# The y product of a Mamba block on small TensorE tiles, with a compact decay matrix and a new layout of PSUM

## The chip, the core and the metric

The kernel runs on one core of one Trainium2 chip. The metric is the device time of one execution in microseconds, as the median of three runs. The profile is of one execution of its own.

A core has five engines with a queue each. TensorE (PE in the profile) does matmuls and loads their weights (PEld). VectorE (DVE) and ScalarE (ACT) do elementwise work and can read PSUM, the memory that matmuls write. GpSimd (POOL) does elementwise work in SBUF alone. SyncE (SP) issues most DMAs. Each queue is served in order; an instruction waits for semaphores of other engines, and what stands behind it waits as well.

## The reference

The input x has 64 sequences of 32 tokens with 512 channels. The first layer adds to x the result of a Mamba block on a conditioned copy of x; the second adds a routed feed-forward layer. The change lies in the Mamba block. Cut to that:

```python
proj = hidden @ in_proj_w.T                  # gate 4096, x 4096, B 1024, C 1024, dt 64
xBC  = silu(causal_conv4(proj.xBC) + conv_bias)
dt   = softplus(dt + dt_bias);  dA = exp(-dt * exp(A_log))
def step(state, t):                          # 64 heads of 64 channels, 8 groups, state size 128
    state = state * dA[t] + dt[t] * x[t] * B[t]
    y[t]  = state @ C[t]
y = y + x * D
y = y * rsqrt(mean_over_group(y * y) + eps) * norm_weight * silu(gate)
out = y @ out_proj_w.T
```

As a sequence has only 32 tokens, the kernel does not step. For each sequence and head it makes a 32 by 32 matrix of decays from token s to token t, multiplies it by the 32 by 32 matrix of B[s]·C[t], and multiplies x by the product.

## The kernel before

The 64 sequences are four tiles T of 16 sequences, so 512 tokens. Channels lie on the partitions and tokens along the free dimension, four blocks bg of 128 tokens (four sequences of 32). For each T the eight groups g are worked through: 32 passes i. All large matmuls are split: each operand is a rounded part (hi) and a rest (lo) in fp32r, and `mm_split` (L159) does hi·hi, lo·hi and hi·lo, 12 matmuls of 128 x 128 x 512 for a product with four blocks of contraction.

The main loop (L689) does the work of three passes at once. For pass i it projects ten chunks of 128 channels (`chunk`, L307: B, C, four of x, four of the gate z): 12 matmuls into a bank with tag "mm", then on ACT and DVE a convolution of four taps (L331, L337), silu (L345), and for x a transpose of 32 x 32 blocks into xs (L349). `x_move` (L404) moves xs by 16 DMAs into xt, with the 128 tokens of a block on the partitions. For pass j = i - 1 it makes the decay matrix: `scan` (L367) on POOL (L372) and DVE (L379); `gram` (L384), 16 matmuls of B and C, each 32 x 32 in the output, whose result DVE multiplies into bd (L397); and `yunit` (L415) four times, the y product. bd is [128 tokens, 4 blocks, 8 heads, 128 tokens]: for each block and head a 128 x 128 matrix whose four diagonal blocks of 32 x 32 are filled (L398) and whose rest was set to zero once (L221). A y product is 8 matmuls with 128 rows of contraction: 4 blocks by 2 heads ("half", 64 channels each).

After the y product DVE adds D·x (L431), ACT squares (L435), POOL sums the squares over c (L439), DVE multiplies by the norm weight and the gate (L442), and ACT and DVE split the result into yhi and ylo (L448, L449). For pass o = i - 2, `sumsq` and `sumsq2` (L453, L462) sum squares over channels and tokens (L457, L459, four small matmuls at L468, L472 on DVE, a power on POOL at L474), `outp` (L493) does the output projection of each block bg by 12 matmuls, and `outp_end` (L509) adds it, scaled, into acc on DVE (L514). `wo_load` (L479) loads and splits the output weights, `w_load` and `w_split` (L287, L295) those of the chunks, with the rests made on POOL (L302, L491). At the first group of a T there are also `cond` (L169, conditioned input), `dt_stage` (L228) and, before it, `attend` (L109). After the last pass follows the feed-forward layer (a convolution, 16 transposes into c2, routing, 16 dense products).

The tile framework decides the order on each engine: it reorders the program's instructions by its own estimates, keeps data dependencies by tile, and sets the semaphores. PSUM has 8 banks, given by tag: three "mm" (chunks), three "yo" (y products, output blocks, and later transposes and half of the dense products), two "gs" (gram and all small results). A tag's banks are used in turn; a writer waits until the bank's last tile has been read.

Of the kernel before, what the change touches and what calls it, by code (L numbers as in the profile page):

```python
# [32 lines left out]
def mamba_block_kernel(  # L33
# [63 lines left out]

    h1_ps = ps.tile([P, NB], F32, tag="gs", name="h1_ps", bufs=2)
# [3 lines left out]
    h2_ps = ps.tile([P, NB], F32, tag="gs", name="h2_ps", bufs=2)  # L102
    nc.tensor.matmul(h2_ps, lhsT=k1["w1"], rhs=h1, start=True, stop=True)
# [5 lines left out]
    def attend(T):  # L109
# [3 lines left out]
        )  # L113
        lg_ps = ps.tile([P, NBG, 8], F32, tag="gs", name=f"lg_ps{T}", bufs=2)
        for bg in range(NBG):
# [53 lines left out]
    def cond(T):  # L169
        acc = acc_of[T]  # L170
        hid = sb.tile([P, 2, KC, TOK], F32R, tag="hid", name=f"hid{T}", bufs=1)
        hid_hi, hid_lo = hid[:, 0], hid[:, 1]
        hid_of[T] = (hid_hi, hid_lo)
        h_of = []
        for k in range(KC):
            h_ps = ps.tile([P, TOK], F32, tag="mm", name=f"h_ps{T}_{k}", bufs=3)
            for bg in range(NBG):
                nc.tensor.matmul(
                    h_ps[:, 128 * bg : 128 * bg + 128],
                    lhsT=acc[:, bg, 128 * k : 128 * k + 128],  # L180
                    rhs=abd[:, bg, :],
                    start=True,
                    stop=True,
                )
            if k == 0:
                b_ps = ps.tile([P, TOK], F32, tag="yo", name=f"b_ps{T}", bufs=3)
# [16 lines left out]
    bd = sb.tile([P, NBG, HPG, P], F32, tag="bd", name="bd", bufs=1)  # L203
    ctxT = const.tile([P, NB], F32, tag="ctxT", name="ctxT")
# [5 lines left out]
    def setup_rest():  # L210
        wdt_s = sb.tile([P, KC, P], F32, tag="dt", name="wdt_s", bufs=1)
        nc.sync.dma_start(out=wdt_s, in_=wdt)
        nc.scalar.copy(wdt_hi, wdt_s)
        nc.vector.tensor_tensor(wdt_lo, wdt_s, wdt_hi.bitcast(F32), ALU.subtract)
        ac = const.tile([P, 2], F32, tag="ac", name="ac")
        nc.vector.tensor_scalar(ac[:, 0:1], k2["alog"], 88.0, None, ALU.min)
        nc.vector.tensor_scalar(ac[:, 1:2], k2["alog"], 88.0, 0.0, ALU.subtract, ALU.max)
        nc.vector.tensor_scalar(ac[:, 1:2], ac[:, 1:2], 80.0, None, ALU.min)
        nc.scalar.activation(e1, ac[:, 0:1], AF.Exp)
        nc.scalar.activation(e2, ac[:, 1:2], AF.Exp)  # L220
        nc.gpsimd.memset(bd, 0.0)  # L221
        ct_ps = ps.tile([P, NB], F32, tag="gs", name="ct_ps", bufs=2)
        nc.tensor.matmul(ct_ps, lhsT=k2["cw"], rhs=k1["condT"], start=True, stop=True)
        nc.vector.tensor_scalar(ctxT, ct_ps, k2["fs"], None, ALU.add)
# [3 lines left out]
    def dt_stage(T):  # L228
# [11 lines left out]
        v, e, s, q, m = (w[:, n] for n in range(5))  # L240
        for r, c in ((slice(0, 64), slice(0, 256)), (slice(64, 128), slice(256, 512))):
            nc.vector.tensor_scalar(v[r], d_ps[r, c], dtb_s[r], None, ALU.add)
        nc.scalar.activation(e, v, AF.Abs)
# [16 lines left out]
        for f in range(2):  # L260
# [3 lines left out]
            )  # L264
        t_ps = ps.tile([P, 2, 2, 64], F32, tag="gs", name=f"t_ps{T}", bufs=2)
        for k in range(2):
# [40 lines left out]
    def chunk(i, c):  # L307
# [38 lines left out]
        if kind == "x":  # L346
            if k == 0:
                st["xs"] = sb.tile([P, NBG, 4, 4, L], F32, tag="xs", name=f"xs{i}", bufs=1)
            nc.vector.transpose(  # L349
                st["xs"][:, :, k].rearrange("p g b c -> p g (b c)"),  # L350
                t.rearrange("p (g x) -> p g x", g=NBG),
            )
# [31 lines left out]
    def gram(i):  # L384
        st = state[i]
        g_ps = ps.tile([P, NBG, L], F32, tag="gs", name=f"g_ps{i}", bufs=2)
        for bg in range(NBG):
            for q in range(4):
                c = slice(128 * bg + 32 * q, 128 * bg + 32 * q + 32)
                nc.tensor.matmul(  # L390
                    g_ps[32 * q : 32 * q + 32, bg, :],
                    lhsT=st[("B", 0)][:, c], rhs=st[("C", 0)][:, c], start=True, stop=True,
                )
        dec = st.pop("dec")
        for q in range(4):
            r = slice(32 * q, 32 * q + 32)
            nc.vector.tensor_tensor(  # L397
                bd[r, :, :, r],  # L398
                dec[r],
                g_ps[r].unsqueeze(2).to_broadcast([32, NBG, HPG, L]),  # L400
                ALU.mult,
            )

    def x_move(i):  # L404
        xs = state[i].pop("xs")
        xt = sb.tile([P, NBG, 4, 4, L], F32, tag="xt", name=f"xt{i}", bufs=2)
        for q in range(4):
            for b in range(4):
                nc.sync.dma_start(
                    out=xt[32 * b : 32 * b + 32, :, :, q, :],  # L410
                    in_=xs[32 * q : 32 * q + 32, :, :, b, :],
                )
        state[i]["xt"] = xt.rearrange("p g c q x -> p g c (q x)")

    def yunit(i, c):  # L415
        g = i % NG
        st = state[i]
        xt = st["xt"]
        y_ps = ps.tile([P, TOK], F32, tag="yo", name=f"y_ps{i}_{c}", bufs=3)
        for bg in range(NBG):  # L420
            for half in range(2):
                nc.tensor.matmul(  # L422
                    y_ps[64 * half : 64 * half + 64, 128 * bg : 128 * bg + 128],
                    lhsT=xt[:, bg, c, 64 * half : 64 * half + 64],
                    rhs=bd[:, bg, 2 * c + half, :],
                    start=True,
                    stop=True,
                )
        cc = 4 * g + c
        y = sb.tile([P, TOK], F32, tag="y", name=f"y{i}_{c}", bufs=3)  # L430
        nc.vector.scalar_tensor_tensor(  # L431
            y, st.pop(("x", c)), dsk_s[:, cc : cc + 1], y_ps, ALU.mult, ALU.add
        )
# [15 lines left out]
        nc.vector.tensor_tensor(  # L449
            st["ylo"][:, c, :], z, st["yhi"][:, c, :].bitcast(F32), ALU.subtract  # L450
        )

    def sumsq(i):  # L453
# [8 lines left out]
    def sumsq2(i):  # L462
        st = state[i]
        part = st.pop("part")
        s_ps = ps.tile([P, NBG], F32, tag="gs", name=f"s_ps{i}", bufs=2)
        pv = part.rearrange("p (g b) -> p b g", b=4)
        for q in range(4):
# [25 lines left out]
    def outp(i, bg):  # L493
# [80 lines left out]
    def c2_tiles(T):  # L574
# [3 lines left out]
        if T == 2:  # L578
            t = sb.tile([P, 2, 4, TOK], F32R, tag="bd", name="c2_2", bufs=1)
            return t[:, 0], t[:, 1]  # L580
        tags = (("acc", 2), ("xt", 2)) if T == 1 else (("yhi", 1), ("ylo", 1))
# [26 lines left out]
    def c2_xpose(j):  # L608
        T, jj = divmod(j, 4)
        c2 = ffn.pop(("c2", j))  # L610
        if jj == 0:
            c2_of[T] = c2_tiles(T)
        o = ps.tile([P, 4, 4, L], F32, tag="yo", name=f"ctp{j}", bufs=3)
        for b in range(4):
# [23 lines left out]
    def route2(T):  # L638
        ls = ffn.pop(("ls", T))
        t_ps = ps.tile([P, NBG, 64], F32, tag="gs", name=f"lt{T}", bufs=2)  # L640
        for bg in range(NBG):
# [162 lines left out]
    dense(2)  # L804
    cnt_ps = ps.tile([64, 2], F32, tag="gs", name="cnt_ps", bufs=2)
    for n in range(16):
# [136 lines left out]
```

## Time and profile before

| | us |
|---|---|
| median of three runs | 1697.29 (1696.21 to 1698.06) |
| span of the profiled execution, first to last instruction | 1693.9 |
| PE busy | 1623.6 |
| DVE busy | 1394.7 |
| POOL busy | 973.9 |
| ACT busy | 791.5 |
| mean granted TensorE clock, share of full | 0.987 |

The profiled execution's own time is not listed apart from its span, which lies 3.4 us under the median of the runs. The page sums busy time by engine, then follows the chain of work that ended last, then lists groups of equal instructions: line, engine, operation, out<-in, shapes and count, then busy us and mean ns of one, then idle time ahead of it and what ended that. The timeline lists instructions in order of time, equal neighbours merged: start, length in us, engine, line. A line of the waits gives who waited for whom, the sum in us, how often, and the longest. A line of the windows gives the stretch and its length, then busy time (count of instructions) of PE, PEld, DVE, ACT and POOL, the granted clock, the busy share of DMA and GB/s.

### The profile page before, as it was taken

How to read it: one execution, taken by the hardware profiler on the slowest of the kernel's cores; microseconds unless marked ns; L12 is line 12 of the kernel's file. 1: busy time of each engine (PE TensorE's matmuls, PEld its weight loads, DVE VectorE, ACT ScalarE, POOL GpSimd, SP SyncE). 2: the span in 40 equal slices, each digit the busy share in tenths (PEclk: the TensorE clock that was granted, in tenths of full speed). 3: DMA queues.
4: the chain of work that ended last, by engine and by line, in shares of the span. 5: the costliest groups of instructions: out<-in, count | busy, mean ns of one | idle time of the engine just before them, and what ended most of it. 6: DMA issues, size and time to landing. Idle time of an engine off the chain costs nothing.

```text
span 1693.9 us, 26413 instructions
## 1 busy us (share of the span) xinstructions
PE 1623.6 (96%) x9427; PEld 1260.1 (74%) x9427; DVE 1394.7 (82%) x1820; ACT 791.5 (47%) x1333; POOL 973.9 (57%) x767
## 2 busy tenths in 40 slices
PE   6899999999999999999999999999999999999999
PEld 5677777777777777777777777777777777777677
DVE  7688888888988788877988878888888878787658
ACT  4444554445545454544645444444644444454330
POOL 5356755654576665564576555665556566665620
PEclk9999999999999999999999999999999999999999
DMA  5344543443555343443554344444344444444333
GB/s 164 91 112 112 135 100 95 111 109 90 110 150 145 92 121 99 111 115 88 125 128 137 100 116 101 108 116 121 86 134 105 120 115 106 118 129 119 100 114 124
DMA packets 376739, 193.70 MB, mean 114 GB/s; under 512 B 285920, under 2 KB 311264, under 8 KB 376608
## 3 DMA queue, kind: packets, MB, share of 16 engines
q1 hardware_dynamic: 375328, 187.81, 43.3%
q0 software_dynamic: 1280, 4.20, 0.6%
q8 instruction: 75, 1.23, 0.3%
q14 instruction: 56, 0.46, 0.1%
HBM read 149.46 MB, written 8.91 MB: 93 GB/s over the span
## 4 chain that ended last, share of the span: by engine, by line
PE 51%; DVE 20%; POOL 12%; issue 8%; DMA 5%; ACT 2%; SPq 1%; POOLq 0%; DVEq 0%; ACTq 0%
PE mm L164 22%; PE o L164 15%; PE y_ps L422 5%; POOL wlo L302 4%; DVE bd L397 3%; POOL wolo L491 3%; POOL y L439 3%; PE fo L164 3%; DVE ylo L449 2%; DMA wor<-in_wout_dram 2%; DVE x L337 2%; DVE z L442 2%; PE cv L164 2%; DMA w<-in_win_dram 1%; DVE src L379 1%
## 5 line engine op out<-in xcount | busy, mean ns | idle before, releaser
L164 PE MATMUL mm<-hid,whi 128*128 128x512 f32 x2560 | 700.8, 403 | 13.5 <-DVE x L337 5.4
L302 POOL TENSOR_TENSOR wlo<-w,whi 128x512 fp32r<-128x512 f32 x320 | 465.8, 1472 | 339.6 <-ACT whi L301 281.0
L164 PEld LDWEIGHTS mm<-hid,whi 128*128 128x128 f32 x2560 | 468.9, 189 | 139.3 <-issue 29.8
L164 PE MATMUL mm<-hid,wlo 128*128 128x512 f32 x1280 | 352.3, 397 | 4.2 <-POOL wlo L302 4.2
L337 DVE SCALAR_TENSOR_TENSOR x<-mm,pack,x 128x496 f32<-128x496 f32 (+2 forms) x384 | 270.2, 708 | 48.2 <-ACT x L331 42.9
L164 PEld LDWEIGHTS mm<-hid,wlo 128*128 128x128 f32 x1280 | 241.9, 189 | 63.9 <-POOL wlo L302 6.8
L491 POOL TENSOR_TENSOR wolo<-wor,wohi 128x512 fp32r<-128x512 f32 x128 | 207.1, 1636 | 11.8 <-ACT wohi L490 10.7
L301 ACT CAST whi<-w 128x512 fp32r<-128x512 f32 x320 | 191.8, 611 | 14.4 <-DMA w<-in_win_dram 10.9
L449 DVE TENSOR_TENSOR ylo<-z,yhi 128x512 fp32r<-128x512 f32 x128 | 143.6, 1122 | 47.3 <-ACT yhi L448 46.1
L442 DVE SCALAR_TENSOR_TENSOR z<-y,pack,z 128x512 f32<-128x512 f32 x128 | 176.4, 1378 | 2.2 <-DVE y L431 0.6
L372 POOL TENSOR_TENSOR src<-dtt,pack 128x256 f32<-128x256 f32 x128 | 75.2, 619 | 165.4 <-DVE bd L397 165.1
L422 PE MATMUL y_ps<-bd,xt 128*64 128x128 f32 x2048 | 165.7, 280 | 1.2 <-DVE acc L514 0.5
L422 PEld LDWEIGHTS y_ps<-bd,xt 128*64 128x64 f32 x2048 | 123.3, 136 | 50.8 <-issue 39.3
L439 POOL TENSOR_TENSOR y<-y,y 128x512 f32<-128x512 f32 x96 | 150.5, 1568 | 16.4 <-ACT y L435 16.3
L397 DVE TENSOR_TENSOR bd<-src,g_ps 32x1024 f32<-32x1024 f32 x128 | 155.3, 1213 | 2.2
L164 PE MATMUL o<-wohi,yhi 128*128 128x512 f32 x512 | 143.9, 400 | 7.8 <-DVE acc L514 4.1
L164 PE MATMUL o<-wohi,ylo 128*128 128x512 f32 x512 | 143.7, 397 | 7.8 <-DVE ylo L449 7.3
L331 ACT ACTIVATE x<-mm,pack 128x512 f32<-128x512 f32 x128 | 99.1, 774 | 96.5 <-PE mm L164 96.5
L328 ACT ACTIVATE z<-mm 128x512 f32<-128x512 f32 x128 | 76.4, 596 | 144.7 <-DVE ylo L449 133.1
L164 PE MATMUL o<-wolo,yhi 128*128 128x512 f32 x512 | 138.8, 393 | 0.0
L345 ACT ACTIVATE x<-x 128x512 f32<-128x512 f32 x128 | 80.2, 628 | 123.7 <-DVE x L337 123.2
L514 DVE SCALAR_TENSOR_TENSOR acc<-o,r,acc 128x512 f32<-128x512 f32 x128 | 93.0, 745 | 46.6 <-POOL r L474 29.7
(190 smaller groups left out, 1755.0 us busy)
## 6 DMA issues: line engine op xcount, KB each, us to landing
w<-in_win_dram SPq DMA_DIRECT2D x320, 256.0 KB, 3.0
wor<-in_wout_dram SPq DMA_DIRECT2D x128, 256.0 KB, 3.1
xt<-xs SPq DMA_DIRECT2D x512, 64.0 KB, 2.3
da<-da SPq DMA_DIRECT2D x128, 128.0 KB, 4.0
acc<-in_x_in_dram SPq DMA_DIRECT2D x4, 1024.0 KB, 7.3
x<-acc POOLq DMA_DIRECT2D x16, 256.0 KB, 2.8
pr<-x SPq DMA_DIRECT2D x64, 64.0 KB, 2.0
x1s<-x SPq DMA_DIRECT2D x16, 256.0 KB, 2.7
```

What stands on the lines that cost most here:

```text
L164: nc.tensor.matmul(o, lhsT=a(k), rhs=b(k), start=j == 0, stop=j == last)
L301: nc.scalar.copy(hi, w)
L302: nc.gpsimd.tensor_tensor(lo, w, hi.bitcast(F32), ALU.subtract)
L331: nc.scalar.activation(t, o, AF.Identity, bias=convb_s[:, cc : cc + 1], scale=convw_s[:, cc, 3:4])
L337: nc.vector.scalar_tensor_tensor(tv[:, :, d:], ov[:, :, : L - d], convw_s[:, cc, 3 - d : 4 - d], tv[:, :, d:], ALU.mult, ALU.add,)
L397: nc.vector.tensor_tensor(bd[r, :, :, r], dec[r], g_ps[r].unsqueeze(2).to_broadcast([32, NBG, HPG, L]), ALU.mult,)
L422: nc.tensor.matmul(y_ps[64 * half : 64 * half + 64, 128 * bg : 128 * bg + 128], lhsT=xt[:, bg, c, 64 * half : 64 * half + 64], rhs=bd[:, b ...
L439: nc.gpsimd.tensor_tensor(y2, st["y2"], y2, ALU.add)
L442: nc.vector.scalar_tensor_tensor(z, y, nw_s[:, cc : cc + 1], z, ALU.mult, ALU.mult)
L449: nc.vector.tensor_tensor(st["ylo"][:, c, :], z, st["yhi"][:, c, :].bitcast(F32), ALU.subtract)
L491: nc.gpsimd.tensor_tensor(lo[:, k, :], w, hi[:, k, :].bitcast(F32), ALU.subtract)
L514: nc.vector.scalar_tensor_tensor(acc[:, bg, :], o, st["r"][:, bg : bg + 1], acc[:, bg, :], ALU.mult, ALU.add)
```

## The change

1. The y product of a block and head is four matmuls, one for each sequence q of the block, with 32 rows of contraction and 32 columns: 32 matmuls per `yunit` where there were 8. Row group q of the array and column half "half" make eight tiles of 32 x 64.
2. The four row groups write to four different banks, so the result of one `yunit` lies in a quarter (128 columns) of each of four banks. Token order follows: q runs slowest in the chunk tokens (hid, B, C, x, z, y), and yhi and ylo are put back into the old order when they are written.
3. bd is gone. DVE multiplies the gram into the decay matrix in place, by one operation of 128 partitions in place of four of 32. The decay matrix gets two buffers (src).
4. PSUM: one tile "quad" of four banks holds y products and output blocks (block bg in bank bg), and by turns (`bank()`) what else had tag "yo". "gs" has one bank where it had two.
5. In the feed-forward part, c2 of tile 2 takes the buffer of xs and a new one, c2x, as bd is gone.

```diff
+    quad = ps.tile([P, 4, TOK], F32, tag="quad", name="quad", bufs=1)
+    turn = [0]
+
+    def bank():
+        turn[0] = (turn[0] + 1) % 4
+        return quad[:, turn[0], :]
...
-            nc.vector.tensor_tensor(h_sb, h_ps, cb_t, ALU.add)
+            nc.vector.tensor_tensor(
+                h_sb.rearrange("p (q g t) -> p g q t", q=4, g=NBG),
+                h_ps.rearrange("p (g q t) -> p g q t", q=4, g=NBG),
+                cb_t.rearrange("p (g q t) -> p g q t", q=4, g=NBG),
+                ALU.add,
+            )
...
-        nc.gpsimd.memset(bd, 0.0)
...
-                st["xs"] = sb.tile([P, NBG, 4, 4, L], F32, tag="xs", name=f"xs{i}", bufs=1)
+                st["xs"] = sb.tile([P, 4, NBG, 4, L], F32, tag="xs", name=f"xs{i}", bufs=1)
...
-        src = sb.tile([P, NBG, HPG, L], F32, tag="src", name=f"src{i}", bufs=1)
+        src = sb.tile([P, NBG, HPG, L], F32, tag="src", name=f"src{i}", bufs=2)
...
-        g_ps = ps.tile([P, NBG, L], F32, tag="gs", name=f"g_ps{i}", bufs=2)
+        g_ps = ps.tile([P, NBG, L], F32, tag="gs", name=f"g_ps{i}", bufs=1)
...
-        dec = st.pop("dec")
-        for q in range(4):
-            r = slice(32 * q, 32 * q + 32)
-            nc.vector.tensor_tensor(
-                bd[r, :, :, r],
-                dec[r],
-                g_ps[r].unsqueeze(2).to_broadcast([32, NBG, HPG, L]),
-                ALU.mult,
-            )
+        dec = st["dec"]
+        nc.vector.tensor_tensor(
+            dec, dec, g_ps.unsqueeze(2).to_broadcast([P, NBG, HPG, L]), ALU.mult
+        )
...
-        y_ps = ps.tile([P, TOK], F32, tag="yo", name=f"y_ps{i}_{c}", bufs=3)
+        yv = quad.rearrange("p q (c g t) -> p q c g t", c=4, g=NBG)
         for bg in range(NBG):
-            for half in range(2):
-                nc.tensor.matmul(
-                    y_ps[64 * half : 64 * half + 64, 128 * bg : 128 * bg + 128],
-                    lhsT=xt[:, bg, c, 64 * half : 64 * half + 64],
-                    rhs=bd[:, bg, 2 * c + half, :],
-                    start=True,
-                    stop=True,
-                )
+            for q in range(4):
+                r = slice(32 * q, 32 * q + 32)
+                for half in range(2):
+                    nc.tensor.matmul(
+                        yv[64 * half : 64 * half + 64, q, c, bg, :],
+                        lhsT=xt[r, bg, c, 64 * half : 64 * half + 64],
+                        rhs=m[r, bg, 2 * c + half, :],
+                        start=True,
+                        stop=True,
+                    )
...
-        nc.scalar.copy(st["yhi"][:, c, :], z)
+        hi, lo = (
+            st[k][:, c, :].rearrange("p (g q t) -> p q g t", g=NBG, q=4) for k in ("yhi", "ylo")
+        )
+        zv = z.rearrange("p (q g t) -> p q g t", g=NBG, q=4)
+        nc.scalar.copy(hi, zv)
...
-        o = ps.tile([P, DM], F32, tag="yo", name=f"o{i}_{bg}", bufs=3)
+        o = quad[:, bg, :]
...
-        tg = ("mm", "yo")[(j + (lo > 0)) % 2]
-        o = ps.tile([P, hi - lo], F32, tag=tg, name=f"fo{j}_{lo}", bufs=3)
+        if (j + (lo > 0)) % 2:
+            o = bank()[:, : hi - lo]
+        else:
+            o = ps.tile([P, hi - lo], F32, tag="mm", name=f"fo{j}_{lo}", bufs=3)
```

The rest of the diff adapts indices and views to the new token order, and sets `bufs=1` for the other tiles with tag "gs".

More of the change, by code (lines that the diff above doesn't have):

```diff
@@ L96, in mamba_block_kernel @@
     convb_s, dsk_s, nw_s, dtb_s = k2["convb"], k2["dsk"], k2["nw"], k2["dtb"]
-    h1_ps = ps.tile([P, NB], F32, tag="gs", name="h1_ps", bufs=2)
+    h1_ps = ps.tile([P, NB], F32, tag="gs", name="h1_ps", bufs=1)
     nc.tensor.matmul(h1_ps, lhsT=k1["w0"], rhs=k1["condT"], start=True, stop=True)
@@ L101, in mamba_block_kernel @@
     nc.scalar.activation(h1, h1_ps, AF.Gelu, bias=k1["b0"])
-    h2_ps = ps.tile([P, NB], F32, tag="gs", name="h2_ps", bufs=2)
+    h2_ps = ps.tile([P, NB], F32, tag="gs", name="h2_ps", bufs=1)
     nc.tensor.matmul(h2_ps, lhsT=k1["w1"], rhs=h1, start=True, stop=True)
@@ L113, in attend @@
         )
-        lg_ps = ps.tile([P, NBG, 8], F32, tag="gs", name=f"lg_ps{T}", bufs=2)
+        lg_ps = ps.tile([P, NBG, 8], F32, tag="gs", name=f"lg_ps{T}", bufs=1)
         for bg in range(NBG):
@@ L185, in cond @@
             if k == 0:
-                b_ps = ps.tile([P, TOK], F32, tag="yo", name=f"b_ps{T}", bufs=3)
+                b_ps = bank()
                 nc.tensor.matmul(
@@ L201, in cond @@
             )
-    bd = sb.tile([P, NBG, HPG, P], F32, tag="bd", name="bd", bufs=1)
     ctxT = const.tile([P, NB], F32, tag="ctxT", name="ctxT")
@@ L220, in setup_rest @@
         nc.scalar.activation(e2, ac[:, 1:2], AF.Exp)
-        nc.gpsimd.memset(bd, 0.0)
-        ct_ps = ps.tile([P, NB], F32, tag="gs", name="ct_ps", bufs=2)
+        ct_ps = ps.tile([P, NB], F32, tag="gs", name="ct_ps", bufs=1)
         nc.tensor.matmul(ct_ps, lhsT=k2["cw"], rhs=k1["condT"], start=True, stop=True)
@@ L240, in dt_stage @@
         v, e, s, q, m = (w[:, n] for n in range(5))
-        for r, c in ((slice(0, 64), slice(0, 256)), (slice(64, 128), slice(256, 512))):
-            nc.vector.tensor_scalar(v[r], d_ps[r, c], dtb_s[r], None, ALU.add)
+        dv = d_ps.rearrange("p (q f g t) -> p f g q t", q=4, f=2, g=2)
+        for r, f in ((slice(0, 64), 0), (slice(64, 128), 1)):
+            nc.vector.tensor_scalar(
+                v[r].rearrange("p (g q t) -> p g q t", g=2, q=4), dv[r, f], dtb_s[r], None, ALU.add
+            )
         nc.scalar.activation(e, v, AF.Abs)
@@ L264, in dt_stage @@
             )
-        t_ps = ps.tile([P, 2, 2, 64], F32, tag="gs", name=f"t_ps{T}", bufs=2)
+        t_ps = ps.tile([P, 2, 2, 64], F32, tag="gs", name=f"t_ps{T}", bufs=1)
         for k in range(2):
@@ L347, in chunk @@
             if k == 0:
-                st["xs"] = sb.tile([P, NBG, 4, 4, L], F32, tag="xs", name=f"xs{i}", bufs=1)
+                st["xs"] = sb.tile([P, 4, NBG, 4, L], F32, tag="xs", name=f"xs{i}", bufs=1)
             nc.vector.transpose(
-                st["xs"][:, :, k].rearrange("p g b c -> p g (b c)"),
-                t.rearrange("p (g x) -> p g x", g=NBG),
+                st["xs"][:, :, :, k].rearrange("p b g c -> p (b g) c"),
+                t.rearrange("p (n t) -> p n t", t=L),
             )
@@ L385, in gram @@
         st = state[i]
-        g_ps = ps.tile([P, NBG, L], F32, tag="gs", name=f"g_ps{i}", bufs=2)
+        g_ps = ps.tile([P, NBG, L], F32, tag="gs", name=f"g_ps{i}", bufs=1)
         for bg in range(NBG):
             for q in range(4):
-                c = slice(128 * bg + 32 * q, 128 * bg + 32 * q + 32)
+                c = slice(128 * q + 32 * bg, 128 * q + 32 * bg + 32)
                 nc.tensor.matmul(
@@ L410, in x_move @@
                     out=xt[32 * b : 32 * b + 32, :, :, q, :],
-                    in_=xs[32 * q : 32 * q + 32, :, :, b, :],
+                    in_=xs[32 * q : 32 * q + 32, b],
                 )
@@ L417, in yunit @@
         st = state[i]
-        xt = st["xt"]
-        y_ps = ps.tile([P, TOK], F32, tag="yo", name=f"y_ps{i}_{c}", bufs=3)
+        xt, m = st["xt"], st["dec"]
+        yv = quad.rearrange("p q (c g t) -> p q c g t", c=4, g=NBG)
         for bg in range(NBG):
-            for half in range(2):
-                nc.tensor.matmul(
-                    y_ps[64 * half : 64 * half + 64, 128 * bg : 128 * bg + 128],
-                    lhsT=xt[:, bg, c, 64 * half : 64 * half + 64],
-                    rhs=bd[:, bg, 2 * c + half, :],
-                    start=True,
-                    stop=True,
-                )
+            for q in range(4):
[8 more added lines that the diff above has]
+                    )
         cc = 4 * g + c
@@ L431, in yunit @@
         nc.vector.scalar_tensor_tensor(
-            y, st.pop(("x", c)), dsk_s[:, cc : cc + 1], y_ps, ALU.mult, ALU.add
+            y.rearrange("p (q x) -> p q x", q=4),
+            st.pop(("x", c)).rearrange("p (q x) -> p q x", q=4),
+            dsk_s[:, cc : cc + 1],
+            quad[:, :, 128 * c : 128 * c + 128],
+            ALU.mult,
+            ALU.add,
         )
@@ L447, in yunit @@
             st["ylo"] = sb.tile([P, 4, TOK], F32R, tag="ylo", name=f"ylo{i}", bufs=1)
-        nc.scalar.copy(st["yhi"][:, c, :], z)
-        nc.vector.tensor_tensor(
-            st["ylo"][:, c, :], z, st["yhi"][:, c, :].bitcast(F32), ALU.subtract
-        )
+        hi, lo = (
+            st[k][:, c, :].rearrange("p (g q t) -> p q g t", g=NBG, q=4) for k in ("yhi", "ylo")
+        )
+        zv = z.rearrange("p (q g t) -> p q g t", g=NBG, q=4)
+        nc.scalar.copy(hi, zv)
+        nc.vector.tensor_tensor(lo, zv, hi.bitcast(F32), ALU.subtract)
     def sumsq(i):
@@ L464, in sumsq2 @@
         part = st.pop("part")
-        s_ps = ps.tile([P, NBG], F32, tag="gs", name=f"s_ps{i}", bufs=2)
-        pv = part.rearrange("p (g b) -> p b g", b=4)
+        s_ps = ps.tile([P, NBG], F32, tag="gs", name=f"s_ps{i}", bufs=1)
+        pv = part.rearrange("p (b g) -> p b g", b=4)
         for q in range(4):
@@ L578, in c2_tiles @@
         if T == 2:
-            t = sb.tile([P, 2, 4, TOK], F32R, tag="bd", name="c2_2", bufs=1)
-            return t[:, 0], t[:, 1]
+            return tuple(
+                sb.tile([P, 4, TOK], F32R, tag=tg, name=f"c2_2_{tg}", bufs=1)
+                for tg in ("xs", "c2x")
+            )
         tags = (("acc", 2), ("xt", 2)) if T == 1 else (("yhi", 1), ("ylo", 1))
@@ L612, in c2_xpose @@
             c2_of[T] = c2_tiles(T)
-        o = ps.tile([P, 4, 4, L], F32, tag="yo", name=f"ctp{j}", bufs=3)
+        o = bank().rearrange("p (b f o) -> p b f o", b=4, f=4)
         for b in range(4):
@@ L639, in route2 @@
         ls = ffn.pop(("ls", T))
-        t_ps = ps.tile([P, NBG, 64], F32, tag="gs", name=f"lt{T}", bufs=2)
+        t_ps = ps.tile([P, NBG, 64], F32, tag="gs", name=f"lt{T}", bufs=1)
         for bg in range(NBG):
@@ L804, in mamba_block_kernel @@
     dense(2)
-    cnt_ps = ps.tile([64, 2], F32, tag="gs", name="cnt_ps", bufs=2)
+    cnt_ps = ps.tile([64, 2], F32, tag="gs", name="cnt_ps", bufs=1)
     for n in range(16):
@@ L815, in mamba_block_kernel @@
     dense(3)
-    r_ps = ps.tile([P, DM], F32, tag="gs", name="r_ps", bufs=2)
+    r_ps = ps.tile([P, DM], F32, tag="gs", name="r_ps", bufs=1)
     nc.tensor.matmul(r_ps, lhsT=crep, rhs=oh, start=True, stop=True)
```

## The prediction

> **What bounds the kernel now.** I read the page's first part, then its chain. TensorE (PE) is busy 96% of the span, VectorE (DVE) 82%, and no other engine comes near.
>
> ```profile
> PE 1623.6 (96%) x9427; PEld 1260.1 (74%) x9427; DVE 1394.7 (82%) x1820; ACT 791.5 (47%) x1333; POOL 973.9 (57%) x767
> PE 51%; DVE 20%; POOL 12%; issue 8%; DMA 5%; ACT 2%; SPq 1%; POOLq 0%; DVEq 0%; ACTq 0%
> ```
>
> The first row does not prove PE the bound, since ends of matmuls are modelled. The timeline of PE alone does: matmul follows matmul.
>
> ```profile
> 819.15 1.09 PE L422 MATMUL y_ps<-bd,xt 128*64 128x128 f32 x16
> 820.17 1.19 PE L164 MATMUL mm<-hid,whi 128*128 128x512 f32 x4
> ...
> 823.15 1.09 PE L422 MATMUL y_ps<-bd,xt 128*64 128x128 f32 x16
> ...
> 835.17 0.46 PE L390 MATMUL g_ps<-C,B 128*32 128x32 f32 x32
> 835.56 1.20 PE L164 MATMUL mm<-hid,whi 128*128 128x512 f32 x4
> ```
>
> Read start to start: a y product takes 820.17 - 819.15 = 1.02 us (16 records, two per fp32 matmul), y product plus chunk 4.00, a gram 0.39 for 32 records. A chunk elsewhere takes 2.79, an output product (outp) 2.73, both read in the same answer. One pass (one group of one token tile) is then 6 x 2.79 + 4 x 4.00 + 4 x 2.73 + 0.4 for the gram + 0.3 for the sums of squares = 44.4 us of PE. The windows between sums of squares of successive passes show 46.2 and 45.7, with DVE busy 39.0 and 37.2:
>
> ```profile
> 500.94:547.10 46.16, 45.85 (x273) 35.72 (x272) 39.01 (x47) 23.80 (x40) 31.21 (x23) 1.00 0.48 129
> 692.30:738.00 45.70, 45.61 (x274) 35.53 (x273) 37.17 (x47) 22.37 (x38) 26.56 (x21) 1.00 0.46 119
> ```
>
> From the first to the last sum of squares there are 31 passes in 1591.0 - 111.8 us, 47.7 each (conditioning, dt stage and attention at the tile boundaries included). So PE sets the pace, and DVE, in strict order and nearly as full, makes the 2 to 3 us of stalls. The timeline of all engines shows how late it runs:
>
> ```profile
> 499.92 1.09 PE L164 MATMUL o<-wolo,yhi 128*128 128x512 f32 x4
> ...
> 506.41 0.15 DVE L472 TENSOR_SCALAR var<-s_ps 128x4 f32<-128x4 f32 x1
> ...
> 506.64 1.03 POOL L474 TENSOR_TENSOR r<-var,mhalf 128x4 f32<-128x4 f32 x1 [1.60 <-DVE var L472]
> ...
> 507.71 0.75 DVE L514 SCALAR_TENSOR_TENSOR acc<-o,r,acc 128x512 f32<-128x512 f32 x1 [1.15 <-POOL r L474]
> ```
>
> The first output block is done on PE at 501.0 and added into acc at 508.5, 7.5 us later. PE did not care: block 1 went into another bank of three. That is the cover which the change removes.
>
> **The change, part by part.**
>
> ```profile
> L397 DVE TENSOR_TENSOR bd<-src,g_ps 32x1024 f32<-32x1024 f32 x128 | 155.3, 1213 | 2.2
> L422 PE MATMUL y_ps<-bd,xt 128*64 128x128 f32 x2048 | 165.7, 280 | 1.2 <-DVE acc L514 0.5
> POOL src L372 <- DVE bd L397: 165.1, 27, 9.4
> ```
>
> *y product.* Per unit 8 matmuls of 128 rows and 128 columns become 32 of 32 rows and 32 columns, 16 records become 64, on 8 array tiles instead of 2. The nearest row is the gram: 32 columns, four tiles of 32 columns, 32 records in 0.39 us, so 12.2 ns a record, or 49 ns for a round of four tiles. The new unit has 8 rounds of 8 tiles. Low end: a round costs as in the gram, 8 x 49 ns = 0.39 us. High end from that row: 64 x 12.2 ns = 0.78. Weights are 64 columns wide, twice the gram's, so I take nearer the high end, 0.70, a gain of 0.32 us per unit, 128 units: 41 us. A rule speaks against it: "TensorE: Matmul & The Clock Gate" of the Trainium skill ("Wait — 56ns, not 53.3ns?") says that start-to-start never falls below about 25 ns however few columns. By the rule a unit is 64 x 25 = 1.6 us, a loss of 0.58 x 128 = 74 us. The gram, 12.2 ns a record, is half that floor, so I follow the row; but no row here has four row groups at once, so the rule's end stays in the range.
>
> *bd.* Four DVE operations of 32 partitions (1.213 us each) become one of 128 partitions with the same 1024 elements per partition: 3 x 1.213 = 3.64 us of DVE less per pass, 116 us in all. In itself it moves nothing, since PE is the bound; it makes DVE earlier. The bd memset (3.5 us of POOL, once) goes.
>
> *src with two buffers.* POOL no longer stands blocked up to 9.4 us behind bd with the weight splits queued behind it. PE waited 11 us for such splits in all, so 0 to 11 us; I take 5.
>
> *PSUM.* The built program shows that every writer of quad waits for the last reader of quad, whichever bank: output block 2 waits for the addition of block 1, y product c+1 for the DVE read of y product c, the first y product for the addition of block 3. Behind the waiting matmul all of PE's queue stands. Three banks in rotation become one. A quad user mostly has one chunk (2.79 us) between it and the next, and in that time DVE must come round. In 9 of the 32 passes the new order puts blocks 1, 2, 3 side by side; each of those two joints costs a bare round trip, about 0.15 + 0.75 (L514) + 0.15 less the normal pitch, 0.9 us: 9 x 1.8 = 16 us.
>
> For the other passes I step through one by hand, in the built order, with the rows' durations (z 1.38, ylo 1.12, the rest about 0.7, bd 1.21). New PE time is 44.4 - 4 x 0.32 = 43.1. Between y reads 1 and 2, DVE has ylo, transpose, z, ylo, read: 5.0 us and 0.7 of waiting for ACT's yhi, against 3.7 on PE; the third y product waits about 0.6, the fourth 0.4. From the end of the fourth y product to the first addition DVE has its backlog 2.5, read 0.73, z 1.38, a wait for POOL's add 0.9, transpose and sum 1.4, ylo 1.1, bd 1.2, six conv steps 4.3, var 0.15, r 1.2, addition 0.75 = 15.6, while PE reaches output block 1 after chunk 3.0, gram 0.4, two chunks 5.6, block 0 2.7, sums 0.3, chunk 2.8 = 14.8: 0.9 us (with joints) of stall. Blocks 2 and 3 have slack. With 0.3 for DMA waits now spread over eight matmuls of the first y product: 2.2 us.
>
> *gs with one buffer.* Three times (passes 9, 17, 25) the gram stands directly behind the sums of squares and must wait for var: about 1.5 us each, 5 us. Elsewhere 8 us of PE lie between: nothing. If that cover went, each would cost the same 1.5.
>
> *Token order.* xs, h_sb, dt, y, yhi and ylo are written with runs of 32 elements. L397 wrote such runs at 1213 ns for 1024 elements, the pace of plain rows, so nothing; the DMA of x keeps its count and its 128-byte destination runs.
>
> Sum per pass: 43.1 + 2.2 stalls, against about 46.0: -0.7 x 32 = -22; joints +16; gram waits +5; POOL -5; the longer passes (47 to 55 us, where DVE's backlog is worst) should give back another 0.5 us on some 25: -13. Together -19 us on the span of 1693.9. The median of runs is 1697.3, 3.4 above that span; so 1678.
>
> **Rivals.** *The lock-step costs more than the matmuls give* (slower). One mechanism: DVE does not come round within one chunk, at the joints y to y and at the first addition. It decides from 2.9 us of stall per pass on (46.0 - 43.1); I have 2.2. At 4 us the sum moves by 1.8 x 32 = 58: 1736. For it: additions are 7.5 us late now; z and ylo show 1.77 us in places. Against: 3.64 us less on DVE. *Small tiles meet a floor per record* (slower): by the rule above 115 us off the sum, 1793; break-even near 13 ns a record. *DVE's relief wins* (faster): if POOL is not in the way z and ylo show 0.75 and 0.7, the lock-step fits, and stalls are under 1 us: 1678 - 1.5 x 32 = 1630. That the change does nothing on PE can also be: if four row groups take turns for weights, the unit stays near 1.0 and the time near 1719.
>
> **How the numbers follow.** My sum (1655 to 1694) 0.45, of which 0.07 lies within 0.2% of before (3.4 us, about what a measurement of this kernel can tell from no change); faster rival 0.13; lock-step 0.27, of which 0.02 within 0.2%; floor or no gain on PE 0.15. Faster 0.51, same 0.09, slower 0.40. Range 1635 to 1745: it leaves out the rule's end and the far ends of both others.
>
> **What would show it.** The y rows should start 64 records within 0.7 us (over 1.0: wrong). bd's row should be x32 at 1.2 us. Among PE's waits y and quad behind DVE L431 and L514 (their new lines) should come up with some 50 to 90 us; over 100 us means that the lock-step rival holds. DVE should be near 1280 us busy. Wrong I am above all if DVE's lag at the joints differs by 1 us, 32 us of time.

## The result, and the profile after

The changed kernel takes 1766.11 us (median of four runs, 1764.15 to 1767.61) against 1696.94 (of four too, 1696.21 to 1698.06): 1.0412 times the time before, with an interval of 1.0397 to 1.0427. It is slower by 69 us; 1678 was predicted, with a range up to 1745. The profiled execution has a span of 1762.4 us, 68.5 above that of before, and a mean granted clock of 0.969 (before 0.987).

First the page's busy times, its chain of work and its row of the y product, then the row of the product that replaced bd.

```profile
PE 1614.7 (92%) x15571; PEld 1256.8 (71%) x15571; DVE 1251.0 (71%) x1724; ACT 805.2 (46%) x1333; POOL 950.6 (54%) x766
...
PE 12%; DVE 6%; issue 5%; POOL 4%; ACT 2%; DMA 2%; SPq 0%; POOLq 0%; ACTq 0%; DVEq 0%
...
L432 PE MATMUL quad<-src,xt 32*64 32x32 f32 x8192 | 123.2, 227 | 48.1 <-DVE y L441 40.6
```

```profile
L408 DVE TENSOR_TENSOR src<-src,g_ps 128x1024 f32<-128x1024 f32 x32 | 38.5, 1204 | 0.1
```

DVE did what was promised: 155.3 us of bd became 38.5, and DVE is busy 144 us less. The y product did too: 165.7 us of PE became 123.2. Yet PE, busy 96% before, is busy 92%: it now stands still more often. The chain's shares add up to 31% of the span only (before, to 99%), so I use the waits instead; POOL's 165 us behind bd are gone from them. The waits of PE say for whom:

```profile
PE quad L171 <- DVE acc L531: 48.1, 42, 3.0
PE quad L432 <- DVE y L441: 40.6, 31, 3.8
PE g_ps L403 <- ACT C L358: 9.5, 3, 4.2
...
PE quad L432 <- DVE acc L531: 5.4, 9, 0.7
```

Three of these lines are waits for the last reader of quad; before, all rows of this kind together were under 5 us. The other line is the gram of three passes, which comes directly behind the sums of squares. It waits for ACT's C, its own operand: DVE had read the sums, and so freed their bank, 0.65 us earlier each time (at 466.94 where C ended at 467.60). Three passes, from sum of squares to sum of squares, show a third effect:

```profile
719.43:767.53 48.10, 46.44 (x465) 36.28 (x464) 35.32 (x46) 23.33 (x38) 26.25 (x21) 0.96 0.48 116
873.31:930.27 56.96, 48.24 (x466) 37.42 (x465) 35.12 (x44) 23.50 (x40) 33.34 (x27) 0.91 0.53 135
1129.59:1175.62 46.03, 44.89 (x466) 35.25 (x465) 33.47 (x42) 21.73 (x36) 26.79 (x21) 1.00 0.45 116
```

The same 466 matmuls cost 44.89 us of busy PE in the third and 48.24 in the second, where the granted clock was 0.91. The mean over 31 passes is 49.8 us, before it was 47.7.

So I split each profiled span into three: idle (span less PE busy), clock loss (half of the busy time that lies in stretches with half the clock), and the rest, which is work at full clock. All three are worked out from the records, and busy ends are modelled.

| profiled execution | span | idle | clock loss | work |
|---|---|---|---|---|
| before | 1693.9 | 70.3 | 17.6 | 1605.9 |
| after | 1762.4 | 147.7 | 49.3 | 1565.4 |
| difference | +68.5 | +77.4 | +31.7 | -40.5 |

The work at full clock shrank by the 41 us that the small matmuls were to give. Idle time took back nearly twice that, and the clock, which had no term in the prediction, another 32.

The first addition, in the timeline of all engines after, beside the one shown of before:

```profile
927.43 1.09 PE L171 MATMUL quad<-wohi,yhi 128*128 128x512 f32 x4
...
931.89 0.15 DVE L489 TENSOR_SCALAR var<-s_ps 128x4 f32<-128x4 f32 x1
...
932.13 1.03 POOL L491 TENSOR_TENSOR r<-var,mhalf 128x4 f32<-128x4 f32 x1 [7.21 <-DVE var L489]
...
933.19 0.75 DVE L531 SCALAR_TENSOR_TENSOR acc<-quad,r,acc 128x512 f32<-128x512 f32 x1 [1.15 <-POOL r L491]
...
934.00 1.20 PE L171 MATMUL quad<-wohi,yhi 128*128 128x512 f32 x4 [0.50 <-DVE acc L531]
```

The addition ends at 933.94, 3.7 us after the sums of squares have followed block 0 (930.27), far less than the 7.5 us of before. These two passes are typical: from the sums to the end of the first addition the median of 32 passes is 7.5 us before and 4.4 after. Still block 1 waits: it starts 0.06 us after the addition.

**How one stall looks.** The timeline of PE around the third y product of a pass, then DVE's in the same stretch:

```profile
904.45 0.86 PE L432 MATMUL quad<-src,xt 32*64 32x32 f32 x64
905.24 1.19 PE L171 MATMUL mm<-hid,whi 128*128 128x512 f32 x4
...
907.20 1.32 PE L171 MATMUL mm<-hid,whi 128*128 128x512 f32 x5
912.29 1.18 PE L432 MATMUL quad<-src,xt 32*64 32x32 f32 x64 [3.77 <-DVE y L441]
913.40 1.65 PE L171 MATMUL mm<-hid,whi 128*128 128x512 f32 x3
914.85 1.91 PE L171 MATMUL mm<-hid,wlo 128*128 128x512 f32 x4
...
918.98 1.20 PE L171 MATMUL mm<-hid,whi 128*128 128x512 f32 x4
```

```profile
904.66 0.68 DVE L350 SCALAR_TENSOR_TENSOR x<-mm,pack,x 128x480 f32<-128x480 f32 x1
905.25 1.38 DVE L457 SCALAR_TENSOR_TENSOR z<-y,pack,z 128x512 f32<-128x512 f32 x1
906.55 0.69 DVE L350 SCALAR_TENSOR_TENSOR x<-mm,pack,x 128x464 f32<-128x464 f32 x1
907.17 2.78 DVE L392 TENSOR_TENSOR_SCAN src<-da,src 128x1024 f32<-128x1024 f32 x1
909.87 0.68 DVE L362 STREAM_TRANSPOSE xs<-x 128x512 f32<-128x512 f32 x1
910.47 1.10 DVE L468 TENSOR_TENSOR ylo<-z,yhi 128x512 fp32r<-128x512 f32 x1
911.50 0.73 DVE L441 SCALAR_TENSOR_TENSOR y<-x,pack,quad 128x512 f32<-128x512 f32 x1
```

The second y product ended at 905.24. Its read (L441) is the last of these DVE rows and ends at 912.23; the third y product starts at 912.29, 0.06 us later. All 31 y products that were held up behind a read start 0.05 or 0.06 us after it ends, so it is this read that releases them. DVE is not idle here: it is 6 us behind, which with three banks in rotation PE need not have noticed. The windows of the same stretch show what follows the stall:

```profile
902.00:908.00 6.00, 6.00 (x87) 4.73 (x87) 4.98 (x7) 4.49 (x8) 4.47 (x4) 1.00 1.00 346
908.00:912.29 4.29, 0.52 (x4) 0.08 (x2) 4.29 (x5) 1.22 (x3) 4.29 (x2) 0.86 0.42 124
912.29:916.00 3.71, 3.71 (x70) 3.16 (x71) 3.68 (x4) 2.78 (x5) 3.54 (x4) 0.50 0.64 132
```

After 3.8 us of idling the clock is 0.50, and four matmuls that otherwise take 0.9 to 1.0 us from start to start take 1.7 (914.85 to 916.55). One stall is paid a second time.

### The profile page after: what moved, and what is told of

It is laid out like the page before. It is cut to its first block, busy times and chain, and to the rows that moved or that the text cites. A ratio compares the mean times of both kernels' runs of the same rounds, so it can differ in the third digit from the quotient of the medians.

```text
span 1762.4 us, 38510 instructions
## 1 busy us (share of the span) xinstructions
PE 1614.7 (92%) x15571; PEld 1256.8 (71%) x15571; DVE 1251.0 (71%) x1724; ACT 805.2 (46%) x1333; POOL 950.6 (54%) x766
## 5 line engine op out<-in xcount | busy, mean ns | idle before, releaser
L171 PE MATMUL mm<-hid,whi 128*128 128x512 f32 x2560 | 718.6, 408 | 6.4 <-ACT whi L314 2.6
L350 DVE SCALAR_TENSOR_TENSOR x<-mm,pack,x 128x496 f32<-128x496 f32 (+2 forms) x384 | 271.6, 710 | 128.9 <-ACT x L344 123.2
L508 POOL TENSOR_TENSOR wolo<-wor,wohi 128x512 fp32r<-128x512 f32 x128 | 203.5, 1607 | 47.7 <-ACT wohi L507 43.8
L171 PE MATMUL quad<-wohi,yhi 128*128 128x512 f32 x512 | 148.9, 413 | 48.8 <-DVE acc L531 48.1
L531 DVE SCALAR_TENSOR_TENSOR acc<-quad,r,acc 128x512 f32<-128x512 f32 x128 | 95.5, 746 | 128.6 <-PE quad L171 95.4
L432 PEld LDWEIGHTS quad<-src,xt 32*64 32x64 f32 x8192 | 108.2, 134 | 98.5 <-DVE y L441 60.6
L432 PE MATMUL quad<-src,xt 32*64 32x32 f32 x8192 | 123.2, 227 | 48.1 <-DVE y L441 40.6
L468 DVE TENSOR_TENSOR ylo<-z,yhi 128x512 fp32r<-128x512 f32 x128 | 131.2, 1025 | 39.1 <-ACT yhi L467 37.8
L171 PEld LDWEIGHTS quad<-wohi,yhi 128*128 128x128 f32 x512 | 93.5, 192 | 85.4 <-DVE acc L531 66.7
L457 DVE SCALAR_TENSOR_TENSOR z<-y,pack,z 128x512 f32<-128x512 f32 x128 | 150.2, 1173 | 2.6
L171 PE MATMUL quad<-wohi,ylo 128*128 128x512 f32 x512 | 144.4, 403 | 0.2 <-DVE ylo L468 0.2
L171 PE MATMUL quad<-wolo,yhi 128*128 128x512 f32 x512 | 140.4, 397 | 0.0
L491 POOL TENSOR_TENSOR r<-var,mhalf 128x4 f32<-128x4 f32 x32 | 32.6, 1020 | 177.4 <-DVE var L489 177.4
```

What stands on the lines that cost most here:

```text
L171: nc.tensor.matmul(o, lhsT=a(k), rhs=b(k), start=j == 0, stop=j == last)
L350: nc.vector.scalar_tensor_tensor(tv[:, :, d:], ov[:, :, : L - d], convw_s[:, cc, 3 - d : 4 - d], tv[:, :, d:], ALU.mult, ALU.add,)
L432: nc.tensor.matmul(yv[64 * half : 64 * half + 64, q, c, bg, :], lhsT=xt[r, bg, c, 64 * half : 64 * half + 64], rhs=m[r, bg, 2 * c + half, ...
L457: nc.vector.scalar_tensor_tensor(z, y, nw_s[:, cc : cc + 1], z, ALU.mult, ALU.mult)
L468: nc.vector.tensor_tensor(lo, zv, hi.bitcast(F32), ALU.subtract)
L508: nc.gpsimd.tensor_tensor(lo[:, k, :], w, hi[:, k, :].bitcast(F32), ALU.subtract)
```

## The experiments

Theory A: the lock-step of the four banks as one tile is the loss, by its waits and the clock that PE loses after them. Theory B, its first rival: small tiles or the new token order slow PE or DVE, and the waits are a symptom. Two more rivals came up on the way: C, PE runs out of instructions; D, the place of DVE's decay scan. The table of all runs comes first; ratios are to before, measured beside them.

| run | median us | ratio (interval) | idle | clock loss | work |
|---|---|---|---|---|---|
| lock_alone | 1865.98 | 1.0994 (1.0968 to 1.1019) | 202.1 | 66.3 | 1589.7 |
| bd_quarter | 1670.72 | 0.9838 (0.9824 to 0.9853) | 56.3 | 11.1 | 1601.4 |
| lock_bd_quarter | 1807.28 | 1.0641 (1.0625 to 1.0657) | 170.5 | 35.6 | 1597.5 |
| gs_one | 1763.15 | 1.0379 (1.0364 to 1.0395) | 119.4 | 41.8 | 1600.9 |
| y_together | 1783.91 | 1.0517 (1.0499 to 1.0535) | 176.8 | 88.3 | 1520.9 |
| out_own | 1737.17 | 1.0238 (1.0223 to 1.0253) | 125.9 | 55.7 | 1555.7 |
| both_free | 1735.67 | 1.0236 (1.0214 to 1.0258) | 140.2 | 55.0 | 1535.4 |
| y_pairs | 1779.45 | 1.0479 (1.0455 to 1.0504) | 171.6 | 62.1 | 1542.9 |
| y_spread | 1812.94 | 1.0671 (1.0635 to 1.0706) | 163.8 | 62.7 | 1585.6 |
| y_spread_z6 | 1856.47 | 1.0947 (1.0930 to 1.0963) | 191.0 | 84.4 | 1578.6 |
| bank_tiles | 1765.97 | 1.0382 (1.0355 to 1.0409) | 84.4 | 74.1 | 1610.0 |
| src_one | 1860.35 | 1.0982 (1.0961 to 1.1003) | 218.1 | 74.4 | 1566.7 |
| s_early | 1744.01 | 1.0288 (1.0271 to 1.0306) | 131.8 | 51.2 | 1559.6 |
| src_one_s_early | 1871.79 | 1.1043 (1.1022 to 1.1064) | 233.3 | 85.3 | 1552.7 |
| late_da | 1794.90 | 1.0592 (1.0559 to 1.0624) | 167.1 | 59.2 | 1565.2 |
| late_da_s_early | 1792.17 | 1.0559 (1.0543 to 1.0575) | 156.6 | 77.1 | 1556.6 |

**The lock-step without the rest.** In the kernel before, with five edits of this kind (all users of the tag "yo"), of which two are shown:

```diff
-        y_ps = ps.tile([P, TOK], F32, tag="yo", name=f"y_ps{i}_{c}", bufs=3)
+        y_ps = ps.tile([P, TOK], F32, tag="yo", name=f"y_ps{i}_{c}", bufs=1)
...
-        o = ps.tile([P, DM], F32, tag="yo", name=f"o{i}_{bg}", bufs=3)
+        o = ps.tile([P, DM], F32, tag="yo", name=f"o{i}_{bg}", bufs=1)
```

> The kernel before, with its 128-row y products and its bd, but one PSUM buffer in place of three for y product, output block and their like, so that each of them waits until DVE has read the one before. Theory A (the lock-step, its waits and the clock that TensorE loses after them, made the change slow): the stalls of the changed kernel (143 us of start-to-start gaps against 64) and its clock loss (55 us against 21) come here too, about +79 and +34, and somewhat more since DVE still has 3.6 us a pass for bd: 1800 to 1860, granted clock 0.97 or lower. Theory B (the small tiles themselves lower the clock, or the new element order slows DVE and ACT, and the waits are a symptom): no small tile and no new order is here, so the clock stays at 0.987 and the time within 1700 to 1730.

It came out at 1866, 6 us above A's range, with no small tile in it and a clock of 0.958. So the waits and the clock come without small tiles, and B is not needed. The 169 us are more than the changed kernel's loss, mostly since DVE still has bd. The next two runs take three quarters of bd away (`for q in range(1)` for `range(4)`), with three banks and with one:

> The kernel before with only the first of the four bd operations of a pass (three quarters of bd stay zero, so y lacks three of four token groups): DVE's relief of 3.64 us a pass alone, with three rotating banks. Theory of the prediction: TensorE sets the pace, so only the longer passes give back some 0.5 us each, 13 us: 1684 (1675 to 1692). Rival (DVE's relief is itself worth much): 1 to 2 us a pass, 1635 to 1665.

> lock_alone (one bank in place of three) with only the first of the four bd operations: the lock-step with the changed kernel's DVE load, but the old y matmuls, two buffers for gram and sums, and one for src. If the lock-step is all of the loss, this is the changed kernel plus the gain of the small matmuls, 0.23 us x 128: 1766 + 29 = 1795 (1780 to 1815), and what it has above bd_quarter is the price of the lock-step, about 110 us. If it is near 1866, DVE's relief does not shorten the lock-step and something else made the changed kernel faster than lock_alone.

They came out at 1671 and 1807, where A had 1684 and 1795: the first lies 4 us below its range, the second within it. The waits of lock_bd_quarter are those of the changed kernel, with the old lines:

```profile
PE o L164 <- DVE acc L514: 68.7, 67, 3.1
PE y_ps L422 <- DVE y L431: 29.7, 20, 4.4
PE g_ps L390 <- ACT C L345: 14.7, 4, 4.6
```

The last line is the gram's wait for C again, here with two buffers for gram and sums: it came with the new order of the instructions, not with the single buffer.

This gives a ladder from before to after: DVE's relief alone 1698 to 1671, -27; the lock-step at that DVE load 1671 to 1807, +137, of which 114 are idle and 25 clock loss by the table; all the rest of the change (small tiles, two src buffers, one gs, token order) 1807 to 1766, -41. That is the main result. The 137 are the price of one buffer together with the order that the framework then builds; no run holds that order fixed.

**One buffer for gram and sums.**

> The kernel before with one buffer in place of two for gram, sums of squares and their like. Theory: in the changed kernel three grams stood 9.1 us behind sums of squares, and two drops of the clock followed; here too, 5 to 15 us: 1702 to 1712. Rival: the order here leaves other work between the two, within 2 us of before.

It cost 65 us, not 5 to 15. The wait, in gs_one:

```profile
PE s_ps L468 <- DVE bd L397: 52.6, 28, 3.2
```

With one buffer the sums of squares wait until DVE has read the gram for bd, four operations of 1.2 us behind its other work. The changed kernel has the same single buffer, and there this wait is 0.3 us: the one product that replaced bd comes early enough. So DVE's relief probably covers this edit, which the prediction did not say; no run has one buffer and the short bd together.

**Taking the lock-step away from the changed kernel.** y_together issues the 128 small matmuls of a pass ahead of the four reads:

```diff
+        if j >= 0:
+            for c in range(4):
+                ymm(j, c)
         for c in range(4):
             if j >= 0:
                 yunit(j, c)
```

out_own gives output blocks the chunks' banks:

```diff
-        o = quad[:, bg, :]
+        o = ps.tile([P, DM], F32, tag="mm", name=f"o{i}_{bg}", bufs=3)
```

> The changed kernel, with all 128 small matmuls of a pass issued ahead of the four DVE reads of y, so that no y product waits for the read of the one before; output blocks stay in the same four banks. Theory A: the gaps ahead of y products, 49.5 us, go, and with them some 14 of the clock drops of 1.7 us each, 25 us: about 1690 (1675 to 1715). Theory B: the clock stays at 0.969, since the small tiles are all there, and the time stays above 1730.

> The changed kernel, with the output blocks in the three banks of the chunks and only the y products in the four banks of quad. Theory A: the gaps ahead of output blocks, 34 + 8 + 5 = 48 us, go, and some 6 drops of the clock, 10 us: about 1708 (1690 to 1730), unless the chunks wait for their banks in turn. Theory B: above 1745, clock 0.97.

> The changed kernel with both: the 128 small matmuls ahead of the four reads, and output blocks in the banks of the chunks. Theory A: what is left is the gain of the small matmuls, 0.23 us x 128 = 29 us, and DVE's relief: 1633 (1620 to 1670), clock 0.985 or better. Theory B: the clock stays near 0.97 and the time above 1700.

All three missed A's ranges: 1784, 1737 and 1736. In y_together and both_free it is B's bet on the time that came true (above 1730, above 1700). It is not B's reason that did: the work at full clock is smaller there than in any kernel with the old matmuls (1520.9 and 1535.4). The waits that each edit was to remove were gone, and new ones had come. In y_together the timeline and the waits of PE show one that names nobody:

```profile
849.22 2.15 PE L431 MATMUL quad<-src,xt 32*64 32x32 f32 x196
857.67 1.15 PE L431 MATMUL quad<-src,xt 32*64 32x32 f32 x60 [6.30 <-issue]
```

```profile
PE quad L431 <- issue: 86.3, 30, 6.3
```

PE stops in the middle of a y product. The DMA queue that carries instructions explains it; the page's third part has it, before and after:

```profile
q8 instruction: 75, 1.23, 0.3%
```

```profile
q8 instruction: 123, 2.02, 0.5%
```

123 transfers of 16,384 bytes for 31,142 records of matmuls and weight loads: 253 a block. The four y products of a pass are 512 such instructions, two blocks, in 3.2 us. In y_together 32 gaps, 87 us in all, lie at ends of blocks, and PE goes on 1.1 to 1.6 us after a block has landed; in both_free there are 19, 49 us. The changed kernel has one, of 0.6 us, as a chunk of 24 instructions in 2.8 us lies between two y products. In out_own and both_free, besides, chunks and output blocks wait for the chunks' banks (38 and 51 us of PE's waits behind ACT's z and DVE's B).

**Spreading and pairing the y products**, output blocks in the chunks' banks:

> As both_free (output blocks in the chunks' banks, the four reads of y behind all 128 small matmuls), but the four y products are no longer in one block: one each behind the chunks x0 to x3. Theory C (in y_together and both_free TensorE ran out of instructions: the trace shows 512 of them in 3.2 us, refilled in blocks of 256 that take 1 us each, and gaps of 2 to 6 us that end 1.2 to 1.6 us after a refill has landed, 87 and 49 us in all): the same instructions, spread over 20 us, leave no such gap: 50 us and some 10 drops of the clock (17 us) less than both_free's 1736: about 1670 (1655 to 1690). Rival (DVE is behind, and the gaps only show it in another place): the gaps move to other instructions, 1715 to 1740.

> Output blocks in the chunks' banks, y products in pairs (0 and 1, two chunks, 2 and 3), each pair's 256 instructions together, its reads behind them. Theory C: a burst is then no longer than one refill block, so the gaps at ends of blocks fall from 49 us to under 12; the second pair waits for the reads of the first, with two chunks (5.6 us) for DVE to come round, so under 15 us of waits: about 1690 (1670 to 1710). Rival (DVE is behind): no better than both_free, 1725 to 1745.

> y_spread with six buffers for the gates z in place of four. In both_free chunks and output blocks waited 36 us for banks whose reader, ACT's Silu of z, had itself waited for a z buffer. If that is the second limit, this run is 20 to 35 us below y_spread; if the buffers only hide DVE's lag, it is within 8 us of it.

The gaps at ends of blocks went (1, none and 2 left), so C holds for them. But the times were 1813, 1779 and 1856: the rival's bet, that DVE is behind and the gaps only move, was right, and more so than it said. In y_spread, then with six z buffers:

```profile
PE mm L171 <- ACT z L341: 77.5, 45, 3.7
```

```profile
PE mm L171 <- DVE B L350: 74.8, 25, 4.2
```

The chunks' banks wait for ACT's z, which waits for a z buffer that DVE frees; with more z buffers the same time is lost behind DVE's convolution of B.

**Four banks as four tiles**, so that an output block waits for its own bank only:

```diff
-    quad = ps.tile([P, 4, TOK], F32, tag="quad", name="quad", bufs=1)
+    quad = [ps.tile([P, TOK], F32, tag=f"quad{n}", name=f"quad{n}", bufs=1) for n in range(4)]
```

> The changed kernel with the four banks as four tiles, so that an output block waits for the readers of its own bank only, and no bank is taken from the chunks; the price is that y is read by four DVE operations of 128 columns in place of one of 512 (about 0.3 us each by 0.15 fixed and 0.15 of the 0.58 that the rest costs: +0.45 us at every y joint). Theory A: the gaps ahead of output blocks, 48 us, and some 6 clock drops, 10 us, go; the y joints, 39 of them stalled, cost 0.45 more, 18 us, and so do later ones: 1715 to 1740. Rival (output blocks wait for something else, the gaps only lie ahead of them): 1765 or more.

1766, the rival's number. But the order changed with it (blocks 1 to 3 side by side, y products cut in pieces that each wait for one read: the row of the y product shows 198.8 us of busy PE, 123.2 in the changed kernel), so the busy time holds waits and the run settles nothing.

**DVE's order.** Six of the long y stalls had the scan (L392, as shown above) between two reads, five more the product L408. src_one sets `bufs=1` for src, late_da moves the load of the decays (`da_load(i)`) from behind chunk 3 to behind chunk 9; both take scan and product out from between the reads of a pass. s_early calls `sumsq2(i)` ahead of `outp(i, 0)`.

> The changed kernel with one src buffer as before. Theory D (the second src buffer lets the planner put DVE's decay scan, 2.78 us, and the product with the gram, 1.2 us, between the reads of y, where the lock-step makes them stalls): with one buffer both come behind the fourth read in the built order. The y joints stalled with a scan or a product between the reads were 1.7 to 4.2 us long, 12 of them, some 24 us, and about 9 drops of the clock went with them, 15 us; POOL's waits for src come back, up to 11: 1735 (1722 to 1750). Rival (my prediction's term: the second buffer is worth 5 us): 1768 to 1778.

> The changed kernel with the sums of squares issued ahead of output block 0 in place of behind it, so that var, r and the first addition can come 2.7 us sooner. Theory: the gaps ahead of output block 1 (34 us behind chunks, 5 behind the gram, each up to 3.4 us) are the lateness of the first addition and mostly go, with 5 or 6 drops of the clock (10 us), unless the sums then wait for DVE's part: 1728 (1715 to 1745). Rival (DVE is late with its own queue and reaches var no sooner): 1755 or more.

> Both edits. Theory: the two add up, about 1697 (1680 to 1715), so that order alone, with the four banks still one tile, takes back what the change lost. Rival: DVE is simply late and the gaps move, 1740 or more.

> The changed kernel, two src buffers, with the load of the decays (da) issued behind the last gate chunk of a pass in place of behind the fourth chunk. The built order then has no scan and no product with the gram between two reads of y of a pass (the changed kernel has 7 and 10), and POOL does not wait for src as it did in src_one. Theory D: the 12 long y joints lose 24 us and their drops of the clock 15: 1727 (1715 to 1745). Rival (DVE is late anyway and the gaps move to the first addition or to a wait for da): 1755 or more.

> Both orders: da late, and the sums of squares ahead of output block 0 (s_early, 1744). Theory D: 1744 less the same 39, 1705 (1690 to 1725). Rival: within 10 us of s_early or above it.

s_early stayed just inside its range: 1744, and waits behind acc fell from 48.1 to 12.9, while the sums now wait for DVE's part (20.1). In the other four theory D missed; the rivals' bets, that DVE is late and the gaps move, came true in three, and src_one lies 82 us above its rival's too. src_one had y joints of 14 us only, but DVE stood behind POOL's src:

```profile
DVE src L392 <- POOL src L385: 77.7, 23, 4.7
```

And late_da, which has neither between the reads and two buffers, keeps the joints as long as they were (40.6 in the changed kernel):

```profile
PE quad L432 <- DVE y L441: 40.5, 25, 3.5
```

So theory D fell: the scan at 907.17 was what DVE happened to be doing, not why it was late. That late_da is 29 us slower than the changed kernel lies for a good part in chunks that wait for their weights (behind ACT's whi, 23.2 us against 2.6). No kernel here that does all the work beats the one before.

## Why the prediction was wrong, point by point

- **PE sets the pace: right.** bd_quarter took 107 us off DVE's busy time (1394.7 to 1287.4) and 27 us off the median.
- **The y product: right in its sum, partly by luck.** 41 us predicted, 42.5 by the rows (165.7 to 123.2). The unit in isolation is 0.79 us start to start (904.45 to 905.24), at the high end of the bounds and not 0.70, so it gains 0.23 us and not 0.32, 29 us in 128. The rest lies in the hand-over, which had no term: by the rows the mean of 128 was 1.29 before, not 1.02, and is 0.96 now. 64 records in 0.79 us are 12.3 ns each, so the rule of 25 ns that the prediction names, which would have given 1.6, does not hold here.
- **bd: right in kind, small in size.** 13 us were put down, 27 came where no lock-step is. With the lock-step the same relief is worth 59 (1866 to 1807).
- **src with two buffers: the term was too small.** src_one shows that the changed kernel needs them: 94 us without. The decay matrix is now the y product's own operand and is held until the fourth product; bd had set it free.
- **Token order: right.** The read takes 730 ns (before 734), z 1173 (1378), ylo 1025 (1122).
- **gs: the waits came, for another reason.** Three grams waited 9.5 us where 5 were put down, but for C and not for var, and with two buffers a gram waits so as well (lock_bd_quarter). What one buffer can cost is the 65 us of gs_one, where DVE is not relieved.
- **PSUM: the step that failed.** "Sum per pass: 43.1 + 2.2 stalls, against about 46.0" makes the lock-step cost 0.6 us a pass net, 19 us, and 40 with joints and gram. lock_bd_quarter against bd_quarter measures 137. Against the predicted -19 on the span, +68.5 is 87.5 off: 55 of it idle time (+77.4, where the sum had 19 + 16 + 5 - 5 - 13 = 22), 32 the clock, nothing the work.

Why the idle term was mis-sized shows in the gaps of PE over 0.6 us from start to start, each less a normal 0.3. The stalls seen were not far above the hand-step: y joints 49.5 us (32 predicted), first addition with its neighbours 40 (29), 9 bare joints of 0.93 us (18 of 0.9), grams 9 (5): 107 in all, where 91 were put down (10 of them for DMA waits). But against them 46.0 - 44.4 = 1.6 us a pass were set as old stalls, 51 us, and 13 and 5 us more that were to vanish. Gaps in the passes of before were only some 33 us, so 36 of these 69 us were not there to be had. With the 16 above, that is 52 of the 55. The 1.6 us were to a good part the y product itself, 1.29 in place of 1.02. So the hand-step came near; what was set against it did not.

The clock had no term at all. The profile of before held it: 13 windows of 3.41 us at half clock, a clock of 0.66 in its worst stretches of 10 us. 33 windows came after, as the new stalls are 2 to 4 us long.

The rival "the lock-step costs more than the matmuls give" is what happened, at 1766 and not 1736: its sign was 94 us on PE and 138 on its weight-load side behind L441 and L531, where "over 100 us" was the mark.

**What stays open.** DVE is busy 71% and yet late: it waits for PE's blocks (95 us), for ACT's x (123) and for POOL (92), and they for it. No run tells which link of that ring sets the lag; removing one moved it. Small tiles with three rotating results were not tried, since a result takes four of eight banks. Nor were four row groups in one bank: the Trainium skill says that different row tiles cannot access the same bank at the same time (TensorEngine Tiling (Array Packing), Restrictions and Gotchas); no run here shows it.

## What to carry to other kernels

Before you trade buffers for faster matmuls, look at how late the reader runs in the profile, not at how busy it is: lateness that rotation hid (7.5 us here) became a stall as soon as a result had one buffer. Price the buffering by an experiment in the old kernel, `bufs=1` for one tag; here it would have shown +169 us before the new matmuls were written. And give the clock a term of its own: of the 20 stretches of 2 us and more in which PE idled in the changed kernel past its first 20 us, 14 had a window of half clock in them or next behind them.

## What the runs showed of the hardware

- **The clock falls after partial idling.** In the traces it is full or half, and it changes on a grid of 3.41 us. Cut on that grid, past the first 20 us, every window in which PE was busy under 0.46 (34 in lock_alone) or 0.49 (6 before, 17 after) was followed by a window of half clock. In the first 20 us this does not hold (a window busy 0.20 at 9.9 us of the changed kernel was followed by full clock), and some busier windows were followed by half clock too. Single gaps between starts of 2.1 us (606.98 to 609.07) and 2.8 us (1314.19 to 1316.97) were enough in the changed kernel. A window at half clock loses up to 1.7 us of work.
- **Instructions can run out.** 512 PE instructions in 3.2 us outran refills of 253, which take about 1.0 us each (median of 123), with 1.1 to 1.6 us to resume behind each landing: 87 us of gaps in y_together.
- **Eight tiles of 32 x 64 at 12.3 ns a record** keep the pace of the gram's four tiles with half the columns of weights.
